# Five-by-five sampling, row maxima and the second norm of a hybrid block: one transfer per tile, maxima through DRAM, and TensorE for part of the sums

## The chip, the cores and the metric

The kernel runs on one core of a Trainium2 chip. The metric is the device time of one execution in microseconds; the time before is the median of three runs. All data is float32 except a few constants in bfloat16.

## The reference, cut to what matters

The input `x` is 8 images of 56 x 56 tokens with 128 channels. Layer 0 is a deformable convolution with a feed-forward part, layer 1 is causal attention within each image, and a layer with 64 experts follows.

```
h      = gelu(batchnorm(depthwise3x3(x)))
offset = h @ w_off                      # per token: 4 groups x 9 points x 2
mask   = softmax(h @ w_msk)             # per token: 4 groups x 9 points
y      = sum over 9 points of mask * bilinear_sample(x @ w_in, point + offset)
y      = y @ w_out
x      = x + gamma1 * layer_norm(y)                       # the first norm
m      = gelu(x @ w_fc1) @ w_fc2
x      = x + gamma2 * layer_norm(m)                       # the second norm
t      = tokens of x;  z = norm(t)
t      = t + softmax(causal(z Wq (z Wk)^T * scale)) @ (z Wv)
t      = t + experts(norm(t))           # each expert takes its 8 best tokens of an image pair
```

Sampling outside the image gives zero. All offsets are smaller than one pixel for these inputs, so that each of the nine points touches at most the places around it, and a token's whole sampling is a weighted sum over a window of 5 x 5 places, with 25 weights for each of 4 groups of 32 channels. (A second, general branch of the program is for larger offsets; a flag decides, and it does not run here.)

## The kernel before, in words

**Groups.** An image's 3136 tokens are 7 chunks of 448, and the chunks form 4 groups: sizes 1, 2, 2, 2 in image 0 and 2, 2, 2, 1 in the others (`sizes`, line 45). A group of two chunks has 896 tokens, which are 7 tiles of 128; one of a single chunk has 3 tiles and a half. There are 32 groups and 200 tiles.

**Lines of work.** Each stage is a Python generator that yields its engine needs and issues instructions: `bring` (load a chunk of x), `prepare` (project it and write it to an image in DRAM), `conv` (depthwise convolution), `plan` (the 25 weights of each token), `fetch` (load the 5 x 5 windows), `weigh` (products), `sums` (25 places to one), `back` (load x transposed), `project` (output projection, both norms, feed-forward), `norm`, `scores`, `maxes`, `keyed`, `exps`, `attend`, `after` (attention), `share` (experts). The string `ORDER` (line 102), one letter per step, fixes in which order the steps of all lines are issued. It was made by a planner from the costs that the `need` calls carry (engine, us, how long until a result is there). When the program runs, these numbers do nothing: each engine takes its own instructions strictly in the issued order and waits on semaphores.

**Sampling.** `prepare` writes `x @ w_in` to `imgs`, two DRAM images of 60 x 60 places with zeroed borders (lines 347 to 354, 527). `fetch` (lines 653 to 669) brings for each token of a tile the 5 x 5 window, 5 runs of 2560 bytes, into one of three buffers `g` of 25 x 128 values per partition. As the rows of the image are 60 wide and a row of tokens is 56, a tile of 128 tokens is cut at each row's end: three or four transfers per tile, all issued by SP. `weigh` (line 692) multiplies the 3200 values by the weights on DVE. `sums` (lines 697 to 718) adds the 25 places on POOL as a tree of six adds: 1536, 768, 384 and three times 128 values per partition; the last frees the buffer. `project` then transposes the result on TensorE (line 762) and copies it from PSUM on ACT (line 764).

**Second norm.** After the feed-forward product `pm` (line 824, tokens on the partitions), `add_normed` (lines 733 to 754) squares and accumulates on ACT (740), takes the power -0.5 on POOL (742, 731), scales each tile on ACT into `ub` (747), transposes it on TensorE into `ptb` (752) and adds it on DVE to `xT` with channels on the partitions (754). The sum is transposed back on TensorE into `pt` (837) and copied to `t` on ACT (842).

**Attention.** For a group, `scores` computes query-by-key products on TensorE (924), and `maxes` reduces each to its row maxima on DVE (947, 949): one value per query, negated, in `neg` with queries on the partitions. The maxima must then stand in one row, row 0 of `qT` (whose channel 0 is free for that), so that the second product, `keyed` (993, keys on the partitions), has the maximum subtracted by TensorE itself. For that `maxes` transposes `neg` piece by piece on TensorE into `pr` (959) and copies it to `qT` on ACT (966). `exps` (1014) and `attend` (1025) follow. The transposed tiles and all temporary products share five PSUM buffers (`gen`, line 263).

Of the kernel before, what the change touches and what calls it, by code (L numbers as in the profile page):

```python
# [8 lines left out]
F32 = mybir.dt.float32  # L9
# [45 lines left out]
def tokens(b, s):  # L55
    return CH * sizes(b)[s]
# [18 lines left out]
def need(engine, us, take=None, give=None, since=None, kind=None, when=None, lock=False):  # L75
# [27 lines left out]
    "pppppppkbbpppwpwbpwwwppwpvkffvfvvvvvvvwvpbwpwccpcccpwcwcccppbccpcccwpcwpcpccvcwvcvcvcvcvcvcv"  # L103
    "cvwggvvvsvvwvwwvwvvsvgvpbpscsspsccsfpgppbpspcpscpscvscvssfvvcvcvcvcsvvcvscscsvcvcvcvvcvsvcfv"
    "cvcgvpbvpcccpvcvpvppbcvpcvcvsgpvgcsvccvscvvssvsvsfmvmpmvpvmvsvgvpbmpsmpscssmpsfmppbmpgmmpsmm"
    "pmmcsmpsmsvscvsfvcgcmscmcvgcsmcscsmsmsfvmkvmnnnnncsvnvvgsnnsnsnsnfcncgnnqcqqcqcxxcxxxcxctcte"
    "ctetaegaecaaccscagooccvsooovoosooscovvvsovsosfovovovovocosvpbopcsopscospsosfoppbpgcpsccosccs"
    "scsspfmpmvmgsmmvvsmvvssmsmsfmgmmsmmmmmsmsvvsssfmgmsmvvgmsmsmskmssfmgmmmmcmsmmsmcmmscmmscmgmm"
    "mscfcccmmcmcmcmcmkmnncnncnnncngcnsnnnccvcncvnvsnvnvgnsvnvnsnvsnsvsfvnvnpnbpqsqxqxqqsqsqsssfc"
    "xcxxxcqxccqxcqxcqqxqxxsqxqxqxsqxspxsgsxfmxmxxmtpstcptgvteetestmtacsaveavemaegsamsasttesfemea"  # L110
    "atmtaemceasvmmvvtsmvmsvtmsmssfamemgstvsmttgsmaeaesaessfaemgaamtctestmeaemakmcaammosmocmoscgm"
    "smcsmcfmomcmmcoocommocmmoomoomoocomccogomcoosmomomoccmokcsmvnnvnngsnnonnossovnovvovsonsfnvnv"
    "nvnnvnconsvononscponbpnsoossnsfvnvpnvcqpqxspvpqbxpqxqsxqxosqxsqcsxfxcmqmgqccqqmxsxqmxqxxqxqx"
    "sqcxqsxqxqsxsqxqsxmqfxcqmqxxqxqxqxcqcmqmcxcmxqxmmcxgcxmmcxpcmxmxpstmgtpmesvvsvamvtvtgessmtet"
    "esmtsftagaemeasmtemstkmasmesamssafemeamgttmetsmttaaesmeamsemssamsfmagamtettseaeteamcamcmcamc"
    "aemsgcsacmtsctemcegstcmsfcetcvcmamacesmaktmstcnncntsncnstncsntnscfaecepcabpagtnpeeetsntpntnt"
    "cnasnaecansnasesengsfanaeenanampnasmpnobpnosmncomcqoqxcoqocqxmxqxqxsqmxsqxssfmxqmqxomxqomocm"
    "oxcopgmmsqmmqcmpqcxpqxcvxqcxqvqxcqxocqgcqsmssxgssfxxxqmvqxqxmoqoqmxoqxqxxqsoxmoxqomoqsqxoxom"
    "sxoqksgosqmsfomqmmxqmxqsxqxqxmxqxqsxmqxsoxsmosqmsfoxmogqmmomsmoqmxmsxomvxsmvxsovssfvvxvxgctv"
    "stetstcvagsvtesvesavesfaevmavtoteooomttsectmgasmeasaesaesmafcvcmcakvcctgctmsemstmteevstcvpcs"  # L120
    "tbscmscpfsnannanenpnnnaeasgetmtstestpstaspsfpeabptagaepeseaaeaspatapststvsevtnfevaevgaemangn"
    "anstnntntnvenvtncvencaevnasveamagctsnesanssnsfmntmqeqxqxqxccqxcqxqcxacxcmcqmmxccqcmmsxgcmmst"
    "mstssccgsfmvccvevvcesvcavmavstvcmtvetvesmtstssfetcmgcaaecaesaevamacscpsqbpctsctsexpcfctpetge"
    "tpctcvtacaecvmevakvaecvaecmvcaaxamcxvomvxmoxctcmvocgtemteamatemeoaatmteameommoaoooaomomootmo"
    "motmemoootmtaomteoamomemoaomokmssonmonnmsnonenmsnonseosanofmoaaomnosmooommnonsmonnnosnmonsms"
    "gosnsfmmncnmnogmcnsonomoconosomvcvcsvscsvcsfvqvmoqxqxqxcmoqcqxsmqxqxcxqocxqxqcqsoxoxmsoxqsom"
    "sqofxomxqkmcomqcmqcomoxcqxmcxqxqxomxqovcmoxcvqocmxocmqovmvqmcxmxcogcxmmvcpmmbxmcxvmgcxpcopmo"
    "tptmoeottetgetptmaaevmeamvemakmsssssnpesntonsfntnbnptnanavepevnavpaevasnavnttnvptsteesaetsae"
    "stnsfnagntntenansgnanensansenssansfeaqqxqxsqxqxqxgmsqmqssmsfqmxsaxxtxtegaesaqqmxqxqsmxsqxqxs"
    "mxsqsfmqxmxgqmmscmmsccmxmvscqscmsqgcfsxcqxqxcqxcgptcbsctptscmescesescfcxcqmcqgttqmaaecqexmcx"  # L130
    "acxaxacmapmopcmocqkmqspnnqnnqnxqxqxnqxxqxsnqxnqxnxnqsxnxmsngpsmnbspsmfonxopxmxpsoqooqxoxcpqx"
    "cqovxqxoqcxqocqxomtxoxtesomtcagoeteqeqsoqsoxqsoxsfoqxoxqoqxoxoqxoqxgsvqxqvosvmoamssovsmvsofv"
    "amvavmxoxmmsgqomosmosqmsqossmfoxxxoosgtmqqseqmqxsxmqsxqsxstfxxtegcexvmsaavmaxsvgmvtkmscstesc"
    "tcfsvtcvtcveacgemamsemamsavtemvctvcstmcsctsecfacetcegtavcacacetctceaecpecmbpacmatcamepcmcmpc"
    "tgmmtmpmtmepmbpamaaemamtpeempampamtkmssvmesvtmvtsevtessvtsfvtvmvavaesaeaesaemasasstmftetsema"
    "gaetaesttetsetgmstmsasmesfagaeaeammsttamnosenntosasenosnensfmotmnonmaomngaeatsnaentoonstonoo"
    "tnosnotsonsaesfegcenanenanscgcnvcscacasvtscvstvsftvemevevnvcovvccgncsanoaoasoqoqcsmtsxxstcft"
    "omgetoaeeqeqvqxxqqmxqcacoomcaomcaxxmpkmxqcbgpcqocmoctmoxepcmcpoxcpocxvaovxovcxovtcxotceoaoot"
    "etvemavavemvtavemtatemeamatameommommotmomootomaoeomooaemtttemetmoaaameamemakmssonmnanmnonmsn"
    "onnosmostssftoetteoaoaeomaooonemonmannmonamnonnogcmnmonommnsccnmncvcmsnvcnomvcvmovovocosvsnv"  # L140
    "sqsfmvqvqxqvxqxoxpmqxbcoqxsmqxqxcomsxqcmgsqpsxqsxsqfovxqxmxpkmompqsmpmxopmscqbqxscqpsqxsmfxq"
    "xqxmqccmqmcxmcxqmxmocpxmcoxomcxgomxcomxomctcmoecgctmctctepcetgpmtaaeaevaevmavtvmetmvtemvtkms"
    "sssstvasnasefnnaennnaenanamomantotevtesnoaoenoaonsoaonotnsoonstonsesfnganentnnetsngneanoaaqs"
    "ooqxsoqxsosoqxsfoqxqoxoqxoqxoxtsogotsoesqeqsqxsxqsfxqxqxqxoxmosgomqqosmqxqsxmqxssxqsxfmxqmax"
    "mgamsmcmsmcgcsomsmvsctsfmcopeombgpsopsmqcspqsxqcmcxqxqcsxcfqxcqxmcqxqxpqcmtmtxexmetckmsssstc"
    "asagecaesacfaqqcaqxsqxqxxqxoxmcnxomspxmbnpgxcosxpmststnsnentmfeotenmgaoaseananmptnngopnocton"
    "otoeoenocootnceqmovgaaesoaoaoqosxoqxosvqosxoqsxosfqvqxqxoxmxovocmvcmvqvmqxsovqxqxcqvsqxoxmso"
    "xsgomsmsfotmqeqxqxsoqqxsxqoxqsooqssqsfxmxxgcqcmcsxqvcqmxcqxsmqxcasxvsxmcstmsfxvmxtvkmvtcevtc"
    "vstecvtevctsgcacsaegsmesamfaemecamgaamttteemaataemveamvacmcpcmmbtgcmcpmctctmmccpmcemcpcececp"
    "pabmaapmttepemapapmtvvtemtevmetvkmsssssvtsvtsfvtvavaetestaaesaesaesasesfattegttstaeaesaeaesg"  # L150
    "asasmasfmntnoennoamnnsnomntotsetgestestsftnoaoaeomgnaeaesnamttoeomnootseonotonansmnaesmesgas"
    "msfmcmnccnmvcocvnavnmnvsvanvonsvmnvosqqmvsqgvsqsfvgmooooosoxoxpxqbpsxqxqscmqxqxxqxcmptxspmst"
    "gftemetetpamvaevaevcavcvacvocmvtkocmocemoacmcoxogcmxcxmotxmtovtecvetcoetmcotocomamaectectaca"
    "ecaeaeaacmacmocmommommotomoomoooetmtttemaetmteomamemtkmssonmnoanamnnsonmennostesaostmnfoaaom"
    "eoetsoamoaooaemeanmansanmonosnonsnsmmngscsfnomnnccnvosgmncocmnsomncsocqososoqxsfqmxqxoqxqcgm"
    "cscvcsxxqsmvsqxsqfoomqoqxomxqxqxoxmoqmoqxomoxqxkmqxocmqmcomxoqcmxqcqomxqxcomxqcxomxqmocxmcvo"
    "xmcvmxvcmxvmxvomcmvtcmvtcgvmcvececgamcatmtoemovavometmomeakmssopooabmpsntnnstnsmnpnesseftptn"
    "pnptbpvmvnaveaevmavsavtteeansateantsesaesnasfgnantnntetemageasmnpnsmpnamnspsnsmnsfnmgmtnmqse"
    "qxqxsqxqsxqsxqsxsfqxqxqxqxqxsaxgmqsmmsqsmqsxsfmxxgscmqccmxqcqvsmcqcsxqcsxsqxsfxqcxmcxpcmqbcm"
    "xpqkscqxcmtsgtxectesctegctcttaaesasegsfaeaeaamqmqacnmsnnnonmqxnxqxoqsnqnxsnqxmqnxqxsmxqsxsfq"  # L160
    "xmxqmqgnmsnnpnsxmoxcqosxcqxpsoxcoqxxpxqxsqsfxqoxqqxxqoxmxcoqmocomxcoqmcoomqgcqcqcompmbpxxgxs"
    "oxogopmsqqomqpqxpsqxsvsxqmsxfqxqxoxoqxoqxosqvoxmomqosxmvoksmxsvmostvsfmoevtvtmgoeomsaaemoqva"
    "sxmqvstostesoootsftegaeceavsaacgscmvtxsmtesctsvsftveaveavecgaccasctctesteccmseacsmcmsvacfvmm"
    "cvamvcmcgtmcvcpmbpcccecpcmacpcxtpmtettgeeaaeatmtxpatbpatepeemptmptmtkmsssssssfvavaevtesvtasa"
    "etesvvvvsmvsasfaeaeaemttsgettstassgaesaesfaeaeagasttetseaeststeassfaeaatamnennnsomnnanntmtoe"
    "tengmoaaesnanstnosntsegtsfneoaenanmcmgsomccomsoomcsoaosvonosotvsfnvmmnvmmngtmotetmsovececosv"
    "oovsonvsasvcnfcgnctntctceacqecaqexacoxqecoqoxcqovcxqvqxqcxqxmcxqxpxabpmgacampcotopctecoctocm"
    "eomeaocmokmcomcamoptotovetetvotvvmvamvavaemveavmttetaemexmamexamaaxamxommotmmomtoemoooooeoam"
    "atmtteeaoamtatoemomtemoakmssonmnoannmsonenmnsonesomsanfaotomntetoooaseoeamnmnaomnanmsnnmmong"
    "csnmmsnsnsmmnsfcgcnmncvcmncvscvvvscvqmovqxoqqxcxoqvcqxcmqxxqsmxqsxsqxsfqxmxqvmqxmsqkxmvmqoxm"  # L170
    "cvmoxpcqboqmxcqxpqmxqcqmsxqxcvqxosxmsqxsmpcfxmooxmomcocooxcommxcommoxomtgcoetcmcecovvacmpacv"
    "ocpvpmvtbvtevmtoaeegmopaattmevmtkomssssssemsftnmgpettmasmpannoanseoenteompnaonaeosantmstosan"
# [2153 lines left out]
```

## Time and profile before

| | us |
|---|---|
| median of 3 runs | 3168.13 |
| lowest and highest of them | 3164.89, 3178.74 |
| the profiled execution's own time | 3183.68 |
| its span, first to last instruction | 3181.9 |
| PE, DVE, ACT, POOL busy | 2810.6, 2210.9, 1629.2, 2292.4 |
| mean granted clock of PE | 0.94 |

The profile comes from the one profiled execution. A busy time is the time in which the engine executes at least one instruction. In a row of a group of instructions stand the source line, the engine, the operation, what it writes and reads by the program's names, the shapes and the count; behind the first bar the busy time in us and the mean duration of one in ns; behind the second bar the idle time of the engine just before these instructions, and what ended it. A matmul's duration includes the time until its result is out, so that consecutive ones overlap; an f32 matmul has two records, a transpose one. "PEld" is the loading of weights. In the windows view a stretch of time has a row: its length, each engine's busy time with the number of instructions, PE's granted clock, the share of time that the DMA engines are busy, and the rate.

### The profile page before, as it was taken

Reading aid. Unit: us, or ns where it says so; the run is one execution under the profiler, and the core shown is the slowest. Engines: PE = TensorE matmul, PEld = TensorE weight load, DVE = VectorE, ACT = ScalarE, POOL = GpSimd, SP = SyncE. Lnnn points to the kernel's source line nnn. Section 1 sums busy time; section 2 is a strip of 40 time slices with the busy share of each in tenths; the row PEclk is TensorE's granted clock in tenths of the full one; section 3 lists DMA queues with packets and bytes.
Section 4 is the critical chain, followed back from the end, with each engine's and each line's share of the span. In section 5 each row is a group of like instructions: output and inputs, shape, how many; then the busy total and the mean of one; then the engine's idle time right before and its main releaser. Section 6 shows DMA issues by size and latency. Waiting matters only on the chain.

```text
span 3181.9 us, 37170 instructions
## 1 busy us (share of the span) xinstructions
PE 2810.6 (88%) x11785; PEld 1620.5 (51%) x11785; DVE 2210.9 (69%) x3887; ACT 1629.2 (51%) x3791; POOL 2292.4 (72%) x2415
## 2 busy tenths in 40 slices
PE   3458899999999999999998999998999999999671
PEld 3334455555555555555555555554555555655331
DVE  6766769777866896678668786687577855466540
ACT  2334565564666456664565556653666455633210
POOL 3878898778876898688858878677568885523543
PEclk7568899999999999999999999999999999999786
DMA  6866778647773787477845867467554857130360
GB/s 167 168 152 147 159 154 180 151 110 168 174 163 80 166 176 160 104 154 170 173 104 112 191 159 168 99 145 155 108 128 100 191 128 148 34 135 12 119 223 26
DMA packets 279862, 442.35 MB, mean 139 GB/s; under 512 B 18977, under 2 KB 132921, under 8 KB 279657
## 3 DMA queue, kind: packets, MB, share of 16 engines
q1 hardware_dynamic: 189352, 382.34, 54.7%
q10 hardware_dynamic: 87040, 51.40, 5.9%
q0 software_dynamic: 3264, 6.15, 0.7%
q8 instruction: 95, 1.56, 0.2%
q14 instruction: 111, 0.90, 0.1%
HBM read 386.03 MB, written 53.95 MB: 138 GB/s over the span
## 4 chain that ended last, share of the span: by engine, by line
PE 57%; DVE 14%; DMA 12%; POOL 9%; ACT 3%; issue 3%; SPq 1%; another core or an unknown queue 1%; ACTq 0%; POOLq 0%; DVEq 0%
PE sc L924 13%; PE av L1025 11%; PE st L993 11%; DMA g<-img 9%; PE ph L812 4%; DVE g L692 4%; PE pm L824 4%; POOL g L708 2%; DVE pv L554 2%; DMA xTd<-xc 2%; POOL g L710 1%; DVE mx L947 1%; PE py L798 1%; PE pg L1097 1%; PE pc L1054 1%
## 5 line engine op out<-in xcount | busy, mean ns | idle before, releaser
L692 DVE TENSOR_TENSOR g<-g,tp 128x3200 f32<-128x3200 f32 (+1 forms) x200 | 696.1, 3482 | 267.4 <-DMA g<-img 184.5
L708 POOL TENSOR_TENSOR g<-g 128x1536 f32<-128x1536 f32 (+1 forms) x200 | 688.9, 3445 | 60.2 <-DVE g L692 53.3
L924 PE MATMUL sc<-zT,qT 128*128 128x512 f32 (+4 forms) x1594 | 625.5, 525 | 18.1 <-DVE mx L947 8.2
L993 PE MATMUL st<-qT,zT 128*128 128x448 f32 (+8 forms) x1606 | 630.5, 513 | 10.2 <-ACT pe L1014 3.9
L1025 PE MATMUL av<-pe,zk 128*128 128x448 f32 (+8 forms) x1606 | 625.1, 513 | 16.3 <-ACT pe L1014 12.8
L1014 ACT ACTIVATE pe<-st 128x448 f32<-128x448 f32 (+8 forms) x803 | 392.1, 504 | 367.0 <-PE av L1025 175.6
L947 DVE TENSOR_REDUCE mx<-sc 128x1 f32<-128x512 f32 (+6 forms) x797 | 439.8, 583 | 97.4 <-PE sc L924 81.4
L924 PEld LDWEIGHTS sc<-zT,qT 128*128 128x128 f32 x1594 | 274.0, 188 | 266.2 <-issue 116.2
L1025 PEld LDWEIGHTS av<-pe,zk 128*128 128x128 f32 (+1 forms) x1606 | 286.3, 192 | 240.2 <-issue 166.2
L993 PEld LDWEIGHTS st<-qT,zT 128*128 128x128 f32 (+1 forms) x1606 | 278.1, 191 | 225.8 <-issue 155.9
L710 POOL TENSOR_TENSOR g<-g 128x768 f32<-128x768 f32 (+1 forms) x200 | 363.5, 1818 | 10.9
L554 DVE SCALAR_TENSOR_TENSOR pv<-xg,dw,pv 128x448 f32<-128x448 f32 x448 | 307.4, 686 | 31.0 <-ACT pv L551 19.8
L812 PE MATMUL ph<-xT,fc 128*128 128x512 f32 (+2 forms) x448 | 221.7, 586 | 24.9 <-DVE xT L754 21.8
L816 ACT ACTIVATE hid<-ph,b_fc 128x512 f32<-128x512 f32 (+2 forms) x224 | 140.8, 634 | 149.1 <-PE ph L812 146.8
L712 POOL TENSOR_TENSOR g<-g 128x384 f32<-128x384 f32 (+1 forms) x200 | 201.4, 1007 | 12.1
L645 POOL TENSOR_TENSOR taps<-taps,a 128x252 f32<-128x252 f32 (+1 forms) x288 | 190.5, 661 | 18.8
L635 POOL TENSOR_TENSOR a<-w 128x756 f32<-128x756 f32 (+1 forms) x96 | 135.8, 1415 | 86.2 <-DVE w L626 77.0
L824 PE MATMUL pm<-fc,hid 128*128 128x128 f32 x1600 | 194.7, 280 | 0.0
L824 PEld LDWEIGHTS pm<-fc,hid 128*128 128x128 f32 x1600 | 184.1, 193 | 11.6 <-issue 11.4
L1231 POOL TENSOR_TENSOR share<-share,part 128x512 f32<-128x512 f32 x56 | 71.0, 1268 | 130.8 <-DVE part L1221 114.0
L742 POOL TENSOR_SCALAR ssb<-ssb 128x4 f32<-128x4 f32 (+1 forms) x56 | 11.7, 208 | 176.3 <-ACT sqb L740 175.8
L812 PEld LDWEIGHTS ph<-xT,fc 128*128 128x128 f32 x448 | 78.4, 200 | 90.3 <-issue 41.1
(259 smaller groups left out, 4213.0 us busy)
## 6 DMA issues: line engine op xcount, KB each, us to landing
g<-img SPq DMA_DIRECT2D x280, 700.0 KB
g<-img SPq DMA_DIRECT2D x56, 600.0 KB
g<-img SPq DMA_DIRECT2D x56, 500.0 KB
g<-img SPq DMA_DIRECT2D x56, 400.0 KB
g<-img SPq DMA_DIRECT2D x56, 300.0 KB
w1t<-in_L_ffn_weight_dram SPq DMA_DIRECT2D x32, 512.0 KB
w2t<-in_L_ffn_weight_dram SPq DMA_DIRECT2D x32, 512.0 KB
xin<-in_x_dram SPq DMA_DIRECT2D x56, 224.0 KB
```

Source lines behind the costliest of these rows:

```text
L554: nc.vector.scalar_tensor_tensor(p3, src, dw[:, k : k + 1], p3, op0=ALU.mult, op1=ALU.add)
L692: nc.vector.tensor_mul(g3, g3, tp[:n, lt % 4].unsqueeze(2).to_broadcast([n, NTAP * NG, 32]))
L708: nc.gpsimd.tensor_add(g[:n, : 12 * C], g[:n, : 12 * C], g[:n, 12 * C : 24 * C])
L710: nc.gpsimd.tensor_add(g[:n, : 6 * C], g[:n, : 6 * C], g[:n, 6 * C : 12 * C])
L712: nc.gpsimd.tensor_add(g[:n, : 3 * C], g[:n, : 3 * C], g[:n, 3 * C : 6 * C])
L812: nc.tensor.matmul(ph[:, :n], fc1[:, f * P : (f + 1) * P], xT[:, :n], start=True, stop=True)
L824: nc.tensor.matmul(four(pm, m)[:, i, :], hid[:, f, i * P : (i + 1) * P], fc2[:, f, :], start=False, stop=i == m - 1 and f == 3,)
L924: nc.tensor.matmul(pp[:w, :n], qT[:, i * P : i * P + w], zTs[b, g][:, k0 : k0 + n], start=True, stop=not diagonal,)
L947: nc.vector.tensor_reduce(mx[:w, i, j : j + 1], pp[:w, :n], AX.X, ALU.max)
L993: nc.tensor.matmul(pp[:w, :n], zTs[b, g][:, j * P : j * P + w], qT[:, u * CH + q0 : (u + 1) * CH], start=True, stop=m <= 0,)
L1014: nc.scalar.activation(pe[:w, :n], pp[:w, :n], AF.Exp, scale=SCALE)
L1025: nc.tensor.matmul(av[:, q0:CH], zs[b, g][:w, j, :], pe[:w, : CH - q0], start=first, stop=last)
```

## The change

1. The DRAM images lose their side borders: rows are 56 wide. A token's window then wraps into the neighbouring row at the sides, but any 128 consecutive tokens lie at one stride, so `fetch` is one transfer per tile. The weights of places that wrapped are set to zero: a constant 0/1 tile `inside`, made at the start from the token's column, multiplies `taps` on POOL at the end of `plan`.
2. `maxes` no longer transposes `neg`. ACT writes it to a DRAM row (one transfer, two where the group has a half tile), and SP reads the row back into row 0 of `qT`.
3. In image 0, `sums` does the first of the six adds on POOL, and TensorE does the rest: 13 matmuls per tile with `g` as the stationary and the identity as the moving operand accumulate 13 places in PSUM. The result comes out transposed, so `project` takes it without a transpose.
4. The second norm leaves tokens on the partitions: `xT` after the first norm is transposed at once (`pt`), and DVE scales `pm` by the power and by a row `grow` of the gains (one instruction per tile), and adds `pt`. `ub`'s scaling on ACT, the transposes `ptb` and the last copies on ACT are gone.
5. The planner's costs are changed in several places, and `ORDER` is another string throughout. The tag of two small tiles changes, and the unused second transposed gain remains.

The diff without `ORDER` and without the lines that only change a cost:

```diff
-    imgs = [indram(f"img{j}", [IW * IW, C]) for j in range(2)]
+    imgs = [indram(f"img{j}", [IW * HW + 4, C]) for j in range(2)]
+    rows_ = [indram(f"maxes{j}", [GT * P]) for j in range(2)]
...
+    column = cst.tile([P, GT, 2], F32, tag="column", name="column")
+    nc.sync.dma_start(column, pos[:, :GT, :])
+    inside = cst.tile([P, GT, 5 * NG], F32, tag="inside", name="inside")
+    nc.vector.memset(inside, 1.0)
+    for k, limit, op in ((0, 2.5, ALU.is_gt), (1, 1.5, ALU.is_gt), (3, 55.5, ALU.is_lt), (4, 54.5, ALU.is_lt)):
+        nc.vector.tensor_scalar(
+            inside[:, :, k * NG : (k + 1) * NG],
+            column[:, :, 0:1].to_broadcast([P, GT, NG]), limit, None, op,
+        )
...
     def plan(b, s):
...
+        yield need(POOL, 0.18 + 0.22 * nt)
+        nc.gpsimd.tensor_mul(
+            taps[:, :nt], taps[:, :nt],
+            inside[:, :nt].unsqueeze(2).to_broadcast([P, nt, 5, 5 * NG]),
+        )
...
     def fetch(b, s):
...
-            t = t0
-            while t < t0 + n:
-                h0, w0 = divmod(t, HW)
-                w = min(HW - w0, t0 + n - t)
-                src = im[h0 * IW + w0 : h0 * IW + w0 + 1, :]
-                src = bass.AP(src.tensor, src.offset, [[C, w], [IW * C, 5], [1, 5 * C]])
-                nc.sync.dma_start(g[t - t0 : t - t0 + w].rearrange("p (r f) -> p r f", r=5), src)
-                t += w
+            src = im[t0 : t0 + 1, :]
+            src = bass.AP(src.tensor, src.offset, [[C, n], [HW * C, 5], [1, 5 * C]])
+            nc.sync.dma_start(g[:n].rearrange("p (r f) -> p r f", r=5), src)
...
     def sums(b, s):
...
+            if idle(b, s):                       # b == 0
+                yT = ys.rearrange("p t c -> p (t c)")
+                yield need(PE, 2.95, take="gen", give="g")
+                pt = gen(f"ptg{b}_{s}_{lt}")
+                for k in (*range(12), 24):
+                    nc.tensor.matmul(pt[:, :n], g[:n, k * C : (k + 1) * C], ident[:n, :n],
+                                     start=k == 0, stop=k == 24)
+                yield need(ACT, 0.15 + 0.00085 * n, give="gen")
+                nc.scalar.copy(yT[:, lt * P : lt * P + n], pt[:, :n])
...
+                continue
...
     def project(b, s):
...
-            yield from add_normed(xT[:, :n], four(pm, m), 1, f"b{nm}_{i0}")
-            yield need(PE, 0.115 * m, take="gen", give="xT")
+            yield need(PE, 0.115 * m, take="gen", give="xT", since=0.0)
             pt = gen(f"pt2{nm}_{i0}")
...
+            ss, u = yield from deviations(four(pm, m), f"b{nm}_{i0}")
+            for i in range(m):
+                nc.vector.scalar_tensor_tensor(u[:, i, :], four(pm, m)[:, i, :],
+                    ss[:, i : i + 1], grow, op0=ALU.mult, op1=ALU.mult)
             full = n // P
-            nc.scalar.copy(t[:, i0 : i0 + full], four(pt, full))
+            nc.vector.tensor_add(t[:, i0 : i0 + full], u[:, :full], four(pt, full))
...
     def maxes(b, s):
...
-        for u in range(N // CH):
-            pr = gen(f"pr{nm}_{u}")
...
-                nc.tensor.transpose(pr[:1, o - u * CH : o - u * CH + w],
-                    neg[r : r + w, i : i + 1], ident[r : r + w, r : r + w])
...
-            nc.scalar.copy(qT[:1, u * CH : (u + 1) * CH], pr[:1, :CH])
+        at = yield need(ACT, 0.45)
+        row = rows_[(NGRP * b + s) % 2]
+        nc.scalar.dma_start(row[: full * P].rearrange("(i p) -> p i", p=P), neg[:, :full])
+        if part:
+            nc.scalar.dma_start(row[full * P : N].rearrange("(p i) -> p i", i=1), neg[:part, full : full + 1])
+        at = yield need(SP, 0.1, since=at + 4.0)
+        nc.sync.dma_start(qT[:1, :N], row[:N].rearrange("(o n) -> o n", o=1))
+        yield need(DVE, 0.0, since=at + 2.6)
```

`deviations` is the first half of the old `add_normed`: the squares with their sums on ACT and the power on POOL. `add_normed` remains for the first norm.

## The prediction

> **What bounds the kernel now.** I read the busy line, then stretches of time, then the groups, then the chain of waits. First the page's busy line:
>
> ```profile
> span 3181.9 us, 37170 instructions
> PE 2810.6 (88%) x11785; PEld 1620.5 (51%) x11785; DVE 2210.9 (69%) x3887; ACT 1629.2 (51%) x3791; POOL 2292.4 (72%) x2415
> ```
>
> PE is the busiest, but 12% of its time is missing. The windows say where (columns: stretch, length, PE, weight loads, DVE, ACT, POOL busy, granted clock, DMA share, GB/s):
>
> ```profile
> 0.00:80.00 80.00, 28.42 (x124) 24.25 (x124) 51.01 (x103) 22.68 (x42) 31.73 (x88) 0.79 0.69 166
> 80.00:160.00 80.00, 34.09 (x140) 24.35 (x141) 61.74 (x74) 29.98 (x71) 68.20 (x72) 0.59 0.82 169
> 160.00:240.00 80.00, 43.91 (x158) 27.29 (x156) 50.45 (x64) 29.30 (x73) 60.57 (x57) 0.63 0.69 155
> 240.00:320.00 80.00, 66.92 (x246) 37.89 (x246) 55.80 (x76) 35.42 (x84) 67.26 (x66) 0.84 0.68 141
> 320.00:400.00 80.00, 68.35 (x287) 40.87 (x286) 62.84 (x117) 41.82 (x97) 67.07 (x69) 0.89 0.71 158
> 400.00:2960.00 2560.00, 2464.55 (x9954) 1412.86 (x9953) 1854.00 (x3252) 1442.45 (x3366) 1899.79 (x1971) 0.99 0.62 137
> 2960.00:3182.00 222.00, 104.35 (x883) 53.02 (x881) 75.05 (x205) 27.52 (x60) 97.76 (x97) 0.74 0.37 130
> ```
>
> PE idles 158 us of the first 400 (400 less 241.7), partly at a low clock; then 95 us of 2560; then 118 us in the expert tail, whose functions the diff leaves alone. So there are two stages to price: the start, where PE waits for image 0's sampling, and the middle, where only PE's own work and stalls count. In the start POOL is busy 68 of 80 us. Its sums are the costly groups (busy, mean ns; then idle before):
>
> ```profile
> L692 DVE TENSOR_TENSOR g<-g,tp 128x3200 f32<-128x3200 f32 (+1 forms) x200 | 696.1, 3482 | 267.4 <-DMA g<-img 184.5
> L708 POOL TENSOR_TENSOR g<-g 128x1536 f32<-128x1536 f32 (+1 forms) x200 | 688.9, 3445 | 60.2 <-DVE g L692 53.3
> L710 POOL TENSOR_TENSOR g<-g 128x768 f32<-128x768 f32 (+1 forms) x200 | 363.5, 1818 | 10.9
> L712 POOL TENSOR_TENSOR g<-g 128x384 f32<-128x384 f32 (+1 forms) x200 | 201.4, 1007 | 12.1
> ```
>
> and the chain of waits just before image 0's last place is summed (303 us) alternates between them and the fetch:
>
> ```profile
> 275.66 3.44 POOL g L708
> 279.17 1.81 POOL g L710
> 281.05 1.01 POOL g L712
> 284.32 14.10 DMA g<-img
> 298.55 3.49 DVE g L692
> ```
>
> So the start is paced by two things together: 7.65 us of POOL per tile (3.45 + 1.82 + 1.01 + three adds of 0.46) and a fetch of over 10 us into three buffers. What the change removes on PE and ACT, by form:
>
> ```profile
> L752 PE MATMUL ptb<-ident,ub 128*128 128x128 f32 x192 | 33.0, 287 | 20.7 <-ACT ub L747 20.7
> L747 ACT ACTIVATE ub<-pm,ssb 128x128 f32<-128x128 f32 x200 | 57.6, 369 | 20.3 <-POOL ssb L731 20.1
> L966 ACT COPY qT<-pr 1x448 f32<-1x448 f32 x56 | 29.0, 518 | 43.0 <-PE pr L959 42.9
> L959 PE MATMUL pr<-ident,neg 128*1 128x128 f32 x168 | 27.9, 272 | 2.5 <-DVE neg L949 1.8 <-ACT yT L764 0.7
> ```
>
> A PE duration includes its drain. Start to start, warm, the trace has 109 ns for one such transpose and 112 ns for each of the two passes of a 128-column f32 matmul (224 ns); I price PE with these.
>
> **What the Trainium skill says.** (1) "DMA: Bandwidth & Descriptors", section "Why a DMA increments its semaphore by 16 and not by 1": a transfer runs on the largest number up to 16 that divides the slowest dimension. The trace agrees: transfers of 56, 40 and 8 tokens show 15, 11 and 9 landing records (14, 10 and 8 engines and the issuer's one), 16 and 32 show 16. (2) The same page, "Two DMAs through the same engine are not ordered": the reader must wait for the writer's semaphore, so the maxima pay two round trips. The trace has the pieces: small ACT-queue transfers (image rows) land in 1.95 us at the 5th percentile, 4.5 at the median, 11 at the 95th (each issue paired with the last landing on its semaphore before that semaphore's next issue). (3) The same page, "Rules for kernel authors": a non-contiguous last dimension becomes one descriptor per element, so a group's maxima are 896 descriptors of 4 bytes; no run shows the cost of such a write. (4) "TensorE: Matmul & The Clock Gate", Part 1: PE is granted half its clock after idling; the windows agree (0.59 at 80-160 us).
>
> **The change, part by part.**
>
> *One transfer per tile.* SP issues 200 fetches instead of 616 (about 0.37 us each, never the limit). Bytes and packets (640 of 2560 B per tile) stay. The busiest engine: a tile of 56+56+16 tokens gives it 20+20+5 = 45 packets, one of 40+56+32 gives 20+20+10 = 50, about 47 on average; with 128 partitions it is 40. A packet takes 193 ns: 9.1 becomes 7.7 us. From first issue to last landing a tile's fetch has a median of 12.4 us; less 1.4, less 0.8 between first and last issue, 10.2. Bounds: 8 (if more engines also speed the packets) and 12.4 (if HBM is the limit). The edges then need a mask: one POOL multiply of 700 elements per group, at 2.24 ns (L708: 3445/1536) 1.6 us, 50 us in 32 groups.
>
> *Image 0's sums.* 25 tiles lose 4.2 us of POOL each, 105 us; POOL's net is -55 us. They gain 13 matmuls of 224 ns, 2.9 us each, 73 us in all, and an ACT copy instead of transpose and copy. To image 0's end POOL needed 25 x 7.65 + 43 of plans (L631, L635 and L645 by form: three groups of 11.8, one of 7.7) = 234 us; now 86 + 43 + 6 = 135, so it paces no more. DMA and DVE (207 us busy to 303 us, unchanged) are next. DMA: 25 x 9.1 + 25 for the rest (the windows' mean share of 0.72 x 303 us, less 25 x 7.7) = 252 us on the busiest engine; the first fetch is issued at 31 us, so 93% of the 272 us to 303 are used. At 25 x 7.7 + 25 = 218 us and the same 93% the end is 265: **38 us earlier**. Below: 10 (packets no faster); above: 75 (8 us fetches).
>
> The matmuls of the first 18 tiles fall where PE idles; those of the last seven fall where it is filling: **+20 us**.
>
> *Maxima through DRAM.* PE loses 224 transposes x 109 ns = 24.4 us, ACT 29 us. A group's first keyed matmul then waits: ACT issues the write, SP waits for it (fetches and x loads stand behind it on SP), issues the read, PE waits for the read; everything on PE stands behind. In the built order of PE I summed what lies between a group's last score and its first keyed matmul: 11 us or more in 17 groups, 7.6 to 9.6 us (8.4 on average) in 13, and 2.1 and 4.4 us in one group each of images 6 and 7. Less 1.2 us for the last reductions, the 13 have 7.2 us of cover, the two 0.9 and 3.2. Round trip: 0.6 to issue + 4.3 write + 0.5 + 3.5 read (x tiles on SP: median 3.1, 5th percentile 2.4) = 8.9. Stalls: 13 x 1.7 + 8.0 + 5.7 = **+36 us**. Bounds: 7 (landings of 1.95 and 2.4 us: a round trip of 5.5) and 129 (both 7 us, behind fetches: 15.1).
>
> *Second norm.* PE loses 200 transposes x 109 ns = 21.8 us, ACT 57.6 of scaling and 29 of last copies (L842); DVE loses 38 (half of L754) and gains 200 x 0.346 (as L1063) + 35 of adds: net +66 us, at nothing, since DVE is 69% busy in the middle; if that cover is gone it costs up to 66. DVE now waits for POOL's power, as ACT did (20 us in 22 waits), with products and maxima queued behind it. PE waits less: 30 us for `pt` on DVE's xT (11.2 + 18.7), 20.7 for `ptb`: I take **-15 us** (0 to -40).
>
> *PE's removed transposes* in the stage that PE paces: 46 us x 0.9 = **-42 us**.
>
> *The new order* moves every engine; I found no price for it other than these, and allow 25 us each way.
>
> Sum: -38 + 20 + 36 - 15 - 42 = -39 us. Against the profiled execution (3183.7: span 3181.9 and 1.8 around it) 3145; the median of the runs, 3168.1, lies 0.5% lower, so the forecast is **3129 us**, by itself 3095 to 3155.
>
> **Rivals.** (A) Both unknowns fall well: fetches of 8 us (start -75) and no stall at the maxima: -75 + 20 + 7 - 15 - 42 = -105, 3063. For it: the matmuls keep PE warm early; against: DVE's 207 us to image 0's end. (B) Packets are limited by HBM, so sixteen engines are no faster: start -10, matmuls on path; -10 + 20 + 36 - 15 - 42 = -11, 3157: no change. For it: 2560-byte packets take 193 ns here while the expert weights' 2048-byte ones take 98, so something other than size slows them. (C) The maxima's round trip takes PE's place as the bound: behind fetches both transfers take 7 us, the stalls are the 129 us above, less the 75 of the other terms: +54, 3222. It decides from a round trip of 11.5 us, where 13 x 4.3 + 10.6 + 8.3 = 75. For it: ACT transfers' 95th percentile is 11 us; against: while SP waits for the write, no new fetch is issued ahead of the read.
>
> **How the numbers follow.** Chances: forecast 0.47, A 0.24, B 0.14, C 0.15. About 0.5% (16 us) is what a measurement of this kernel tells from no change. Faster: the forecast's and A's, 0.71; same: B's, 0.14; slower: C's, 0.15. The range reaches from A's time to between B and C, 3060 to 3185.
>
> **What would show it.** Image 0's last weighing near 262 us (was 299); the three small POOL adds 175 times instead of 200; a fetch near 10 us; PE idle in the first 400 us near 100; PE's waits for the row read about 36 us in all. Waits over 75 us there would make C right; fetches of 12 us would make B right; a DVE over 80% busy in the middle would break the free second norm.

## The result, and the profile after

The changed kernel takes 3153.59 us (median of 6 runs, 3151.01 to 3156.76), the kernel before beside it 3170.48 us (6 runs). The ratio is 0.9942, interval 0.9922 to 0.9961: a gain of 0.6%, 17 us, small but clear of the noise. The forecast was a gain of 39 us. The direction held, but the experiments show that two of the forecast's three largest terms, the fetch (-38) and the maxima (+36), were wrong by far more than the sum is, in opposite directions.

The profiled run of the changed kernel took 3155.84 us. Its busy line:

```profile
span 3154.0 us, 37084 instructions
PE 2799.6 (89%) x11986; PEld 1655.0 (52%) x11986; DVE 2264.0 (72%) x4101; ACT 1497.9 (47%) x3489; POOL 2235.8 (71%) x2322
```

The span is 27.9 us shorter than before. PE is busy 11 us less and idle 17 us less (354.4 where it was 371.3): almost nothing, for a change of five parts. The windows show why (columns as before: stretch, length, PE, weight loads, DVE, ACT, POOL busy, granted clock, DMA share, GB/s):

```profile
0.00:80.00 80.00, 34.62 (x193) 31.32 (x194) 52.12 (x109) 25.47 (x49) 29.58 (x80) 1.00 0.61 178
80.00:160.00 80.00, 60.28 (x389) 48.62 (x388) 63.62 (x94) 32.06 (x80) 59.53 (x57) 0.87 0.61 214
160.00:240.00 80.00, 66.62 (x433) 55.38 (x432) 71.18 (x80) 39.23 (x100) 55.49 (x41) 0.89 0.63 218
240.00:320.00 80.00, 72.67 (x369) 48.24 (x368) 67.15 (x93) 37.17 (x99) 60.66 (x52) 0.94 0.57 190
320.00:400.00 80.00, 71.30 (x300) 41.70 (x299) 65.90 (x124) 36.61 (x83) 58.66 (x63) 0.96 0.48 144
400.00:2960.00 2560.00, 2410.65 (x9487) 1385.77 (x9487) 1885.29 (x3431) 1306.79 (x3034) 1881.72 (x1942) 0.97 0.42 132
```

In the first 400 us PE now idles 94.5 us (it was 158), at a clock of 0.87 and more in the second and third window where it was 0.59 and 0.63. Between 400 and 2960 us it idles 149 us where it was 95, and the clock fell from 0.99 to 0.97. So the start was won and the middle lost. The idle time that came in addition stands before one line, the keyed matmuls. This is their group before the change, and then, after it, the same group with the weighing and the first GpSimd add (busy, mean ns; then idle before):

```profile
L993 PE MATMUL st<-qT,zT 128*128 128x448 f32 (+8 forms) x1606 | 630.5, 513 | 10.2 <-ACT pe L1014 3.9 <-DVE st L521 2.1 <-ACT t L842 1.8
```

```profile
L707 DVE TENSOR_TENSOR g<-g,tp 128x3200 f32<-128x3200 f32 (+1 forms) x200 | 694.7, 3477 | 100.8 <-DMA g<-img 78.4
L1047 PE MATMUL st<-qT,zT 128*128 128x448 f32 (+8 forms) x1606 | 664.1, 537 | 114.5 <-DMA qT<-maxes 99.5
L726 POOL TENSOR_TENSOR g<-g 128x1536 f32<-128x1536 f32 (+1 forms) x200 | 690.4, 3452 | 94.1 <-DVE g L707 85.6
```

Before, the keyed matmuls had 10.2 us of idle time in front of them and a mean of 513 ns; now 114.5 us, of which 99.5 us wait for the row of maxima, and 537 ns. DVE's waits for a fetch fell from 184.5 to 78.4 us. Issues paired with their landings (as in the prediction) give: the row's write lands 9.1 to 14.6 us after its issue (median 10.9; 4.3 had been assumed), its read after 1.3 to 6.4 (median 2.5; 3.5 assumed), a tile's fetch after a median of 6.8 us (10.2 assumed, 12.4 before).

The write does more than keep PE waiting: fetches that move beside it are late too. This is the chain of waits inside the changed kernel around one row write, issued at 568.6 us and landed at 580.7 (columns: start, us, what):

```profile
568.82 0.46 POOL ys L754
569.28 0.02 issue
569.30 16.97 DMA g<-img
586.27 0.03 issue
...
586.37 3.49 DVE g L707
```

A fetch issued 0.7 us after the row's write took 17 us instead of 6.8. Its packets of 2560 bytes can be counted by microsecond: 74 of its 640 start before 580 us; from 581 us on, when the write has landed, packets of fetches start at 112 to 162 in each microsecond. Of the 200 fetches, 15 are under way together with a row write for more than 2 us; their median is 13.2 us, that of the other 185 is 6.7. There is a second way: SP, which issues the fetches too, waits for the write before it issues the row's read, 601 us in all, and the fetches next in its order stand behind that wait.

### The profile page after: what moved, and what is told of

It reads as the page before. It is cut to its first block, busy times and chain, and to the rows that moved or that the text cites. A ratio compares the mean times of both kernels' runs of the same rounds, so it can differ in the third digit from the quotient of the medians.

```text
span 3154.0 us, 37084 instructions
## 1 busy us (share of the span) xinstructions
PE 2799.6 (89%) x11986; PEld 1655.0 (52%) x11986; DVE 2264.0 (72%) x4101; ACT 1497.9 (47%) x3489; POOL 2235.8 (71%) x2322
## 4 chain that ended last, share of the span: by engine, by line
PE 65%; DVE 12%; DMA 11%; POOL 6%; issue 3%; ACT 2%; ACTq 0%; SPq 0%; POOLq 0%; DVEq 0%
PE sc L982 16%; PE st L1047 15%; PE av L1079 14%; DMA maxes<-neg 7%; PE ph L857 4%; PE pm L869 3%; DVE g L707 3%; DMA g<-img 2%; DVE pv L568 2%; POOL g L726 1%; DMA qT<-maxes 1%; DVE mx L1005 1%; PE py L843 1%; PE pg L1151 1%; PE pc L1108 1%
## 5 line engine op out<-in xcount | busy, mean ns | idle before, releaser
L707 DVE TENSOR_TENSOR g<-g,tp 128x3200 f32<-128x3200 f32 (+1 forms) x200 | 694.7, 3477 | 100.8 <-DMA g<-img 78.4
L1047 PE MATMUL st<-qT,zT 128*128 128x448 f32 (+8 forms) x1606 | 664.1, 537 | 114.5 <-DMA qT<-maxes 99.5
L1079 PE MATMUL av<-pe,zk 128*128 128x448 f32 (+8 forms) x1606 | 617.0, 510 | 3.1 <-ACT pe L1068 2.0
L1047 PEld LDWEIGHTS st<-qT,zT 128*128 128x128 f32 (+1 forms) x1606 | 289.9, 199 | 358.4 <-issue 246.5
L746 POOL TENSOR_TENSOR g<-g 128x768 f32<-128x768 f32 (+1 forms) x175 | 317.9, 1817 | 8.9
L857 PE MATMUL ph<-xT,fc 128*128 128x512 f32 (+2 forms) x448 | 214.5, 572 | 23.6 <-DVE xT L795 23.1
L748 POOL TENSOR_TENSOR g<-g 128x384 f32<-128x384 f32 (+1 forms) x175 | 175.4, 1002 | 11.1
L778 POOL TENSOR_SCALAR ssb<-ssb 128x4 f32<-128x4 f32 (+1 forms) x56 | 11.2, 199 | 179.1 <-ACT ub L776 161.9
```

Source lines behind the costliest of these rows:

```text
L707: nc.vector.tensor_mul(g3, g3, tp[:n, lt % 4].unsqueeze(2).to_broadcast([n, NTAP * NG, 32]))
L746: nc.gpsimd.tensor_add(g[:n, : 6 * C], g[:n, : 6 * C], g[:n, 6 * C : 12 * C])
L857: nc.tensor.matmul(ph[:, :n], fc1[:, f * P : (f + 1) * P], xT[:, :n], start=True, stop=True)
L1047: nc.tensor.matmul(pp[:w, :n], zTs[b, g][:, j * P : j * P + w], qT[:, u * CH + q0 : (u + 1) * CH], start=True, stop=m <= 0,)
L1079: nc.tensor.matmul(av[:, q0:CH], zs[b, g][:w, j, :], pe[:w, : CH - q0], start=first, stop=last)
```

## The experiments

Each row of this table is a kernel of its own, timed beside the kernel before on the same chip. The chips differ between rows, so rows are compared by their ratios, which are to the kernel before; the kernel after stands at 0.9942. In e2 and e13 the row doesn't come back in its right places; they are there for the timing alone.

| run | what it is | us, before beside it | ratio, interval |
|---|---|---|---|
| e1 | after, maxima by PE transposes again | 3048.2, 3185.8 | 0.9568, 0.9548 to 0.9589 |
| e2 | after, row written in 28-byte runs | 3004.1, 3185.8 | 0.9426, 0.9401 to 0.9451 |
| e6 | after, one transpose, 512-byte rows | 3009.6, 3185.8 | 0.9450, 0.9431 to 0.9469 |
| e5 | after, image 0 summed on GpSimd | 3231.7, 3185.8 | 1.0144, 1.0119 to 1.0168 |
| e8 | before, with the fetch part alone | 3091.4, 3183.9 | 0.9704, 0.9680 to 0.9728 |
| e9 | e6, fetch cut in pieces of 56 | 3215.2, 3183.9 | 1.0100, 1.0075 to 1.0125 |
| e10 | e6, fetch cut in halves of 64 | 3087.7, 3183.9 | 0.9694, 0.9668 to 0.9719 |
| e7 | e6, second norm as before | 3095.9, 3183.9 | 0.9719, 0.9695 to 0.9743 |
| e11 | e8, only image 0 in one transfer | 3159.6, 3173.2 | 0.9956, 0.9939 to 0.9974 |
| e12 | e8, only images 1 to 7 in one transfer | 3098.2, 3173.2 | 0.9762, 0.9746 to 0.9778 |
| e13 | after, maxima written 64 bytes apart | 2989.0, 3173.2 | 0.9415, 0.9397 to 0.9433 |
| e14 | e13, and read back from there | 3048.8, 3187.2 | 0.9571, 0.9552 to 0.9591 |

**The maxima's way.** The theory: the late write ate the gain. The rival: PE waits there, but something else would have ended last anyway. First the PE transposes come back (e1):

```
-        nc.scalar.dma_start(row[: full * P].rearrange("(i p) -> p i", p=P), neg[:, :full])
-        nc.sync.dma_start(qT[:1, :N], row[:N].rearrange("(o n) -> o n", o=1))
+        nc.tensor.transpose(pr[:1, o - u * CH : o - u * CH + w], neg[r : r + w, i : i + 1], ident[r : r + w, r : r + w])
+        nc.scalar.copy(qT[:1, u * CH : (u + 1) * CH], pr[:1, :CH])
```

> The kernel after, with the group's maxima brought to the row by PE transposes and ACT copies again; all else stays, the order string too (the two transposes stand where the row's read and its landing stood). Theory (the maxima's round trip is what ate the gain: its write lands after 9 to 14 us, where 4.3 had been assumed, and PE waits 99 us for the row): 99 us of waits go, 224 transposes x 109 ns = 24 us of PE come back, so about 75 us less than the kernel after: 3080 us, and no wait of the first keyed matmul over 1 us on average. Rival (PE was not the bound where it waited; fetch or exponentials end last there): under 20 us less, 3135 us or more, with PE's waits moved to another line.

Measured: 0.9568, about 119 us less than after ((0.9942 - 0.9568) x 3170), though PE gets its 224 transposes back. The theory holds, and its 75 us were too few. Next, the same transfers and the same waits with another size of piece (e2). A group of seven tiles is then written in runs of 28 bytes; the 64 values of a half tile, a second write in eight groups, stay single values of 4 bytes:

```
-            row[: full * P].rearrange("(i p) -> p i", p=P), neg[:, :full]
+            row[: full * P].rearrange("(p i) -> p i", p=P), neg[:, :full]
```

> The kernel after, with the row written in runs of 28 bytes (each partition's seven maxima side by side, 128 runs for a group) where it was 896 single values of 4 bytes; the row that comes back then has its places in another order, so the maxima stand at the wrong tokens. Same transfers, same waits. In the trace of the kernel after, a write of 64 values lands as late (9.3 to 10.2 us) as one of 896 (9.1 to 14.6), and the last 4-byte packet has moved 1.5 us after the issue. Theory 1 (the count of values is no cost; a small piece is slow to be confirmed): landing stays at 8 us or more, 3145 to 3155 us. Theory 2 (the count of pieces makes the landing late): landing under 4 us, PE's waits for the row under 20 us, 3075 us.

Measured: 0.9426, 3004 us and well below the 3075 of theory 2, with a median of 3.5 us over all the writes. That median mixes kinds: the runs of 28 bytes land after 1.9 us, the runs of 12 bytes in the eight shorter groups after 3.3, and those groups' writes of 64 single values, on the same queue, after 7.8 (6.8 to 10.6). So theory 2's signs came true, but not for its reason: 64 pieces are later here than 128 longer ones, and in the kernel after 384 values land after 9.8 us where 896 take 11.5. The count of pieces is not the main cost. The version that keeps the maxima in their places with long rows is e6 (its step is put off where no PSUM buffer is free):

```
+        nc.tensor.transpose(pr[:nt, :P], neg[:, :nt], ident)
+        nc.scalar.copy(short[:nt], pr[:nt, :P])
+        nc.scalar.dma_start(row[: nt * P].rearrange("(i p) -> i p", p=P), short[:nt])
```

> The kernel after, with one PE transpose of a group's maxima (128 x 7 to 7 x 128), an ACT copy, and the write of 7 rows of 512 bytes; the read stays. If pieces of 4 bytes make the write late (theory), it lands like the image's 512-byte rows do, 2 to 5 us, the round trip is about 0.7 + 0.1 + 3.5 + 0.3 + 2.7 = 7.3 us against a cover of 7.2 us in 13 groups and more in 17, waits 10 to 25 us, PE work +3.5 us: 3070 to 3085 us. Rival (any write to DRAM on this queue with a wait behind it takes 9 us here, because other transfers are ahead of it): landing 9 us or more, 3155 us.

Measured: 0.9450, well beyond the 3070 to 3085 us expected. The write lands in 1.6 us (median), the read in 1.5. Its page's busy line, and its group of keyed matmuls:

```profile
span 3006.2 us, 37172 instructions
PE 2758.5 (92%) x12018; PEld 1635.2 (54%) x12018; DVE 2259.8 (75%) x4109; ACT 1504.4 (50%) x3521; POOL 2237.6 (74%) x2322
```

```profile
L1049 PE MATMUL st<-qT,zT 128*128 128x448 f32 (+8 forms) x1606 | 630.3, 514 | 7.8 <-DVE st L535 2.5 <-DVE om L601 2.3 <-ACT pe L1070 1.5
```

Against the kernel after, the span is 147.8 us shorter: 106.7 us of it PE idle (354.4 against 247.7), and 41.1 us PE busy, though e6 has 32 transposes more. 34 of those 41 us are this one line, 664.1 against 630.3 us for the same 1606 matmuls. Between 400 and 2750 us the clock is 0.97 in after and 1.00 in e6: the trace's clock records have PE at half clock for about 140 us of that stretch in after, in 22 spells of which 13 lie about the end of a wait for the row, and for 20 us in e6. So by these two runs a stall of about 5 us on PE costs about a third more than it shows (34 us on 107), an estimate. Fetches beside a row write are no longer late either (17 overlap with one at all; their median is 6.6 us, as for the others), and SP waits 349 us for the writes instead of 601. The remaining question was what makes the 4-byte write late; e13 keeps the pieces and their number, and puts each 64 bytes from the next:

```
-            row[: full * P].rearrange("(i p) -> p i", p=P), neg[:, :full]
+            row[: full * P * 16].rearrange("(i p x) -> p i x", p=P, x=16)[:, :, 0], neg[:, :full]
```

> The kernel after, with each of a group's maxima written 64 bytes from the next, as 4-byte pieces still; what comes back for the row is then mostly zeros, so the exponentials are taken without their maxima. It parts two readings of the late write: if several engines writing into the same 64 bytes is what delays it, the landing falls under 5 us and the time to about 3010 us (0.945 to 0.955); if a 4-byte piece is late by itself, the landing stays over 8 us and the time near 3154 us (0.99).

Measured: the landing's median is 2.8 us and the time 0.9415. Pieces of 4 bytes are not late by themselves; they are late side by side. The expectation's reading, several pieces within the same 64 bytes, fits but isn't shown: 64 bytes is the only spacing tried, it also spreads the row over sixteen times the addresses, and e2's runs of 28 bytes share 64 bytes too, two or three at a time, and land after 1.9 us. Reading the spread values back (e14, with `row[: N * 16].rearrange("(o n x) -> o n x", o=1, x=16)[:, :, 0]` as the read's source):

> The kernel after, whole, with the maxima written 64 bytes apart and read back from there (896 pieces of 4 bytes in the read as well). The write should land in about 3 us, as in the run with the same write and another read (median 2.84 us); the read of scattered values should land in 2 to 5 us (1.5 us for a contiguous row). Round trip about 7 us or less: 2990 to 3020 us, 0.942 to 0.951, so the kernel with 64-byte spacing beats the kernel before and the kernel after. If scattered reads land as late as the 4-byte writes side by side did (9 us or more), the waits return and the time is 3100 us or more.

Measured: 0.9571, a miss. The scattered read lands after 6.3 us (median; a contiguous row 1.5), PE waits 28.1 us for it, so part of the stall returns. e6 is the version to keep: the row is right, and it beats both kernels.

**Image 0's sums.** e5 sums image 0 with the six GpSimd adds again, inside the changed kernel's order (the adds stand where the matmuls stood):

```
-                for k in (*range(12), 24):
-                    nc.tensor.matmul(pt[:, :n], g[:n, k * C : (k + 1) * C], ident[:n, :n], start=k == 0, stop=k == 24)
+                nc.gpsimd.tensor_add(g[:n, : 6 * C], g[:n, : 6 * C], g[:n, 6 * C : 12 * C])
+                ...
```

> The kernel after, with image 0's places summed by the six GpSimd adds and transposed by PE, as for the other images; all else stays. Prediction's pricing (the matmuls cost 20 us of PE's path, POOL's relief is a part of the 38 us): POOL needs 25 x 7.65 + 43 + 6 = 240 us to image 0's end, so the last weighing of image 0 moves from 274 us to 280 to 290, and the time by -20 + 15: within 10 us of the kernel after. Rival 1 (the 73 us of matmuls lie on PE's path almost whole, so the change gave back there what the start had won): 40 us less or more, 3110 us. Rival 2 (POOL bounds the start): 30 us more, 3185 us.

Measured: 1.0144, 64 us slower than after, twice what rival 2 said: without the matmuls POOL paces the start. Its windows (same columns) show PE starved again and POOL busy 76 of 80 us:

```profile
160.00:240.00 80.00, 43.77 (x168) 28.47 (x169) 55.23 (x65) 27.55 (x69) 75.73 (x73) 0.64 0.50 170
240.00:320.00 80.00, 42.45 (x170) 27.67 (x170) 53.24 (x76) 25.73 (x73) 76.90 (x77) 0.66 0.54 187
```

Image 0's last weighing ends at 331 us, with the matmuls at 274, before at 347. It is a hard undoing, since the order string was made for the matmuls, and the late row weighs more in it (PE waits 117.7 us for the row, 99.5 in after); what stands is that the faster fetch alone does not free the start.

**The fetch.** e8 puts the first part alone into the kernel before, with its order, sums, maxima and norm (the tile of squares, of which only the sums are used, becomes bfloat16):

> The kernel before with the first part of the change alone: image rows 56 wide, one transfer for a tile's places, and the mask multiply (run in the last of the plan's GpSimd steps); sums, maxima, norm and order string of before. Theory (formed from the run with image 0 summed on GpSimd, whose last weighing of image 0 came at 331 us though its fetches took 7 us): POOL paces the start, so the faster fetch alone buys little: fetch from 12.4 to about 7 us, image 0's last weighing from 347 to 325 to 335 us, the time 10 to 25 us less than before, 0.992 to 0.997. Rival (the prediction's view, that the fetch is the bound and POOL's sums close behind): last weighing at 310 us or earlier, 38 us or more gained, 0.988 or less.

Measured: 0.9704, 92 us. The theory missed. The rival's 38 us or more came true, but not its reason: image 0's last weighing, at 317 us, is 31 us earlier than before where it asked for 37, and the time fell by three times those 31 us. The fetch alone does better than the whole change. Where the gain lies, e11 and e12 tell, with `w = min(HW - t % HW if b > 0 else P, t0 + n - t)` as the length of a piece, and with `b == 0`:

> The kernel before with the first part of the change (56-wide image rows and the mask), where only image 0 is fetched in one transfer a tile; images 1 to 7 are fetched in pieces of 56 and less, as before. With one transfer everywhere that kernel stood at 0.970. Theory (the prediction's step that a faster fetch is worth something in the start alone is wrong: by the copies of the attention sums the gain was 35 us at image 1's end and 91 us at image 7's): a gain of 20 to 45 us, 0.986 to 0.994. Rival (the start's lead is what all the later gain rests on): 0.970 to 0.976.

> The reverse: image 0 fetched in pieces of 56 and less, images 1 to 7 in one transfer a tile. Theory: the rest of the 0.970, a gain of 45 to 75 us, 0.976 to 0.986, with PE's waits of the middle (for the normed tokens, the exponentials, the x tiles) shorter than before. Rival: little, 0.990 or more.

Measured: 0.9956 for image 0 and 0.9762 for images 1 to 7, 14 us (less than the 20 to 45 expected) and 75 us, together nearly e8's 92. The start is the small part, though e11's last weighing of image 0, at 318 us, is as early as e8's. In the middle a late fetch holds DVE, and with DVE's queue the maxima, norms and copies that PE waits for. This path is read from the waits; the two runs show only where the time lies. DVE's waits between 400 and 2750 us, before and then e12 (columns: us in total, times, longest):

```profile
DVE g L692 <- DMA g<-img: 154.8, 56, 9.7
```

```profile
DVE g L705 <- DMA g<-img: 18.8, 8, 7.9
```

PE's own busy time in that stretch rises from 2255.9 to 2303.8 us of 2350, and its idle time halves. PE's waits for other engines shrink, such as this one of the kernel before (same columns and stretch), which falls to 1.4 us:

```profile
PE av L1025 <- ACT pe L1014: 12.8, 8, 7.1
```

Why is the fetch so much faster? e9 and e10 cut it again, in e6, where no late row write hides it:

```
+            while t < t0 + n:
+                w = min(HW - t % HW, t0 + n - t)      # e9;  min(64, ...) in e10
```

> The version with one transpose and 512-byte rows for the maxima, its fetch cut at the image's rows again (pieces of 56, 40, 16 and so on, three or four transfers a tile, from the same 56-wide image). Theory (a transfer whose partitions spread over all sixteen engines is what shortened the packets from 193 to 119 ns): packets back to 170 ns or more, fetch 10 to 12.5 us, image 0's last weighing from 270 to 295 us or later, 20 to 50 us slower than that version, 0.95 to 0.96. Rival (the even spread is only worth the busiest engine's 47 to 40 packets, 1.4 us, and the fetch is not on the path once POOL is relieved): under 8 us slower.

> The same version with the fetch cut in two halves of 64 partitions: twice the transfers, each over sixteen engines. If the spread over the engines decides and not the number of transfers: packets near 119 ns, a fetch of 7 to 7.5 us, within 6 us of that version (0.943 to 0.947). If the number of transfers decides: fetch 9 us or more, 15 us slower or more.

Measured: e9 1.0100, e10 0.9694, against e6's 0.9450. Both are slower by far more than the theory expected. e10 refutes the spread over the engines: its transfers run on sixteen engines too, and its packets take 197 ns all the same (e9 192, e6 115). A tile's fetch takes 10.8 us in it, where e10's other reading, the number of transfers, asked for 9 or more. One window of e10 and the same of e6, 80 to 160 us (same columns), show the DMA engines busy 94% where 64% sufficed for more bytes:

```profile
80.00:160.00 80.00, 61.96 (x386) 51.43 (x385) 62.30 (x87) 31.82 (x79) 54.45 (x48) 0.85 0.94 199
```

```profile
80.00:160.00 80.00, 63.46 (x411) 51.88 (x410) 65.14 (x96) 34.52 (x88) 59.71 (x58) 0.88 0.64 232
```

But the number of transfers isn't it either: in e6 the eight tiles of 64 tokens, one transfer each, land after 6.3 us (median), the 128-token tiles after 6.6. Half the bytes take nearly the same time. What these runs leave is the number of partitions that a transfer covers. The Trainium skill has this: "SBUF — State Buffer", section "Door 1: The DMA port swizzle", says that partitions 0 to 63 reach only eight of SBUF's sixteen DMA ports, and gives 196 GB/s measured for 64 partitions. The trace agrees: while packets of fetches are moving, e10's fetches move 197 GB/s, those of before 174, e6's 309. If the ports are the limit, sixteen engines share eight of them, and a packet should take about twice as long (an estimate from that section); the medians are 209 ns in e10 and 102 in e6. The port itself isn't seen in a trace; that the rate follows the partitions is.

**The second norm.** e7 puts the old norm back into e6 (ACT scaling, transposes, DVE's multiply-add, transposes back, ACT copies in the steps of the new order):

> The same version with the second norm of before (ACT scaling, PE transposes to channels on the partitions, DVE's multiply-add, PE transposes back, ACT copies), written into the steps of the new order: 200 more PE transposes, 86 us more on ACT, some 105 us less on DVE. The prediction's price, -22 for the transposes and -15 for the waits: 37 us slower than that version, 0.957. Rival 1 (the waits that the new norm saved were the larger part: 63.5 us before, 27 after): 55 us slower or more, 0.963. Rival 2 (DVE's relief gives it back, since DVE is 75% busy): under 15 us slower, 0.949.

Measured: 0.9719, 86 us slower than e6: rival 1, and more. PE is idle 33 us longer than in e6 and busy 52 us longer. Its PE groups show the transposes of the scaled tokens, and those back:

```profile
L886 PE MATMUL ptb<-ident,ub 128*128 128x128 f32 (+1 forms) x200 | 40.9, 289 | 19.4 <-ACT ub L882 18.2 <-DVE mx L1004 0.8
L892 PE MATMUL pt<-ident,xT 128*128 128x128 f32 (+1 forms) x200 | 34.5, 291 | 19.8 <-DVE xT L887 19.1
```

That is 39 us of waits before the two lines and 41 us of busy time in the added transposes (`ptb`). Here too the steps weren't placed for the old norm, so 86 us is what it costs in this order; what it cost in its own, no run shows.

## Why the prediction was off, step by step

**One transfer per tile (-38).** Two things failed. The price of 40 packets at 193 ns each kept the packet's duration and shortened only the busiest engine's list; packets fell to 119 ns, because the 193 came from narrow transfers (e10), and the fetch took 6.8 us, beyond the bound of 8 that the prediction set. And the step priced the start only: for the middle the prediction held that "only PE's own work and stalls count", so DVE's 155 us of waits for fetches there were priced at nothing. e12 puts 75 us on them, e11 14 us on the start. The prediction also misread one instant: the weighing that ends at 302 us is the 21st tile's; by the tiles' order on DVE, image 0's 25th and last ends at 347.5, so its sum for the start, which has all 25 tiles done at 303, rests on the wrong end.

**Image 0's matmuls (+20).** Right in mechanism: PE takes them mostly where it idled (94.5 us idle in the first 400, "near 100" predicted). But their price stood alone, while the gain of what they relieve was booked to the fetch. Undone in the new order, their lack costs 64 us. Together the two terms were to win 18 us; image 0's last weighing came 74 us earlier (347.5 to 273.8), 31 of them with the fetch alone (e8).

**Maxima through DRAM (+36).** This term failed by the most. The path was right: a write, SP's wait, a read, and all of PE behind it; it is rival C's mechanism, and its sign of over 75 us of waits came in (99.5), though not its loss of time. The size was wrong in the piece that no trace showed: the write was priced by the image's rows (4.3 us, at worst 7), which are 512 bytes long. It took 10.9. With the transposes that it takes off PE (-22), the part was to cost 14 us; against PE's transposes put back (e1) it cost 119. Against the cheap row of e6 it is 148 us of span: 107 of idle time, the fetches that stood behind the write among its causes, and 41 of longer PE busy time, most of it the clock. The waits alone stayed under the bound of 129, but that bound is itself too low: it lets only 15 groups wait, and with its round trip of 15.1 us the other 17, with a cover of 9.8 or more, can wait as well. The profile shows PE waiting for the row in 19 of the 32. The skill had hints: the page "DMA: Bandwidth & Descriptors", in its specifications, says that below 512 bytes a transfer does read-modify-write, and the section "Back-pressure in remote DMA" (told there of remote transfers) says that stalled writes stall an engine's other queues. The first doesn't give the price: 28-byte runs land after 1.9 us and 4-byte pieces 64 bytes apart after 2.8, both under 512 bytes, where 512-byte rows take 1.6. With the second the runs agree in kind, for a write that is not remote: fetches beside a 4-byte write take 13.2 us instead of 6.7. Whether it is that mechanism, no run shows.

**Second norm (-15) and the removed transposes (-42).** The signs were right. In e7 the norm with its own 200 transposes is worth 86 us, where -15 and half of -42 made 36. DVE's added work shows no cost that outweighs this; DVE is busy 74% of the middle, under the 80% named as a sign. (It was 72% before, not the 69% that the prediction gives, which is the whole span's. And its 30 us of waits for `pt` add 18.7 us of the weight loads' waits to 11.2 of PE's own.)

**The sum.** Rivals A and C each held for one part, at the same time; the prediction gave each of them a chance, and none to both together. A fetch that gains more than A's 75 (92 us alone, in the old order) and a row that costs more than C's 129 (148 by e6) work against each other. That a sum built on two such terms came within 22 us of the gain is luck. The parts are not additive: everything but the whole-tile fetch is slower than the kernel before (e9, 1.010), the fetch alone gives 0.970, all with a cheap row 0.945. The order is fixed, so a transfer that lands late holds up what stands behind it on the engine that waits for it, and what other engines need from there.

What stays open: how much of e5's and e7's loss is the part undone and how much its place in an order made without it; what the new order is worth by itself, for which the prediction allowed 25 us each way and which no run sets apart; and why 4-byte pieces side by side are late, and up to which spacing.

## What to carry to other kernels

Price a new transfer by a row with the same size of piece and the same neighbours, not by the same queue's average; where no row shows it, a transfer that a whole engine waits for deserves an upper bound of several times the nearest one. In a kernel with a fixed order, an engine's waits for a transfer are not free because another engine is the bound: look for what stands behind them in its queue. Before splitting a transfer, count the partitions that each piece covers.

## What the runs showed of the hardware

- A write to DRAM of 4-byte pieces side by side from 128 partitions landed after 9.1 us or more in the kernel after (medians: 896 pieces 11.5 us, 384 pieces 9.8; in e2, 64 pieces from 64 partitions 7.8); of the write at 568.6 us the last 4-byte packet had been moved 1.5 us after the issue. The same pieces 64 bytes apart land after 2.8 us, runs of 28 bytes after 1.9, rows of 512 bytes after 1.6 (medians).
- While such a write is unfinished, fetches on the other queue crawl too: 13.2 us for those beside it for more than 2 us, 6.7 for the others; beside e6's 512-byte rows, 6.6.
- A fetch to 64 partitions takes as long as one of twice the bytes to 128 (6.3 and 6.6 us); in halves, a 128-token tile took 10.8 us.
- 896 scattered 4-byte reads into one partition land after 6.3 us, the contiguous row after 1.5.
- A stalled PE loses clock besides time: 1606 equal matmuls took 664 us behind 114 us of stalls, at a clock of 0.97 in the middle, and 630 us behind 8 us of them, at 1.00.
